# Attention of two sequences' same heads issued as couples: five full score groups instead of six, and a new order of the steps around them

## The chip, the cores and the metric

The kernel runs on one core of a Trainium2 chip. The metric is the device time of one execution in microseconds (us): 2496.99 us is the median of three runs, from 2496.44 to 2498.13. PE is the matrix engine (PEld its weight loads), DVE the vector engine, ACT the scalar engine, POOL the GpSimd engine, SP the engine whose queue issues all the transfers here.

## What is computed

The input is x of shape 8 x 512 x 1024 (eight sequences of 512 tokens), all in float32.

```
x = x + layernorm(attention(layernorm(x)))
x = x + layernorm(x' @ weight.T + bias + lora(x')),   x' = layernorm(x)

attention: 16 heads of 64; q, k with rotary embedding; causal mask
logits = q k^T / sqrt(64); attn = softmax(logits); out = attn v; out @ Wo
```

The change concerns the softmax part only: scores, exponentials, normalisation, transposition of the probabilities, and their product with the values.

## The kernel before

All large products (q and k, v, Wo, the feed-forward weight) are done with a seven-product scheme for 2 x 2 blocks (`PRODUCTS`, `GROUPS`). The kernel has four stages: values for all sequences; the q and k projections with attention beside them; the output product; the feed-forward product. The middle stage is the one that the change touches.

**Ticks.** The middle stage has eight units (`u` = 0 to 7: a group of 8 heads times two sequences). A unit has 49 ticks (`N2`). In each tick PE does one product of the projection, four matmuls of 256 columns (8 records in the trace, L636), and the accumulators are drained by DVE and ACT one tick later (`drain`, L116, L118, L125). Everything else is put on the ticks by `at(tick, fn, kind)`. `run` (L177) sets the order inside a tick: first all "pe" entries in the order in which they were registered, then the projection's product with its drain, then all other entries and the "post" entries, again as registered. Every engine's queue is in that written order. `plan_unit` registers ahead of the attention of the same unit.

**plan_unit** puts on DVE and POOL the sums that finish the projection (`add_cu`, L654) and the rotary embedding (`rotate`: L672 and L675 on DVE, L678 on POOL, then transfers to `qk`, L687). For units 1 to 6 the DVE sums stand on ticks 43 (A += D, first half), 44 (D += E first half, A += D second half), 45 (D += E second half), 50 and 51; the DVE steps of `rotate` on ticks 38 to 41, 46 to 49, 52 to 55 and 57 to 60, the POOL steps on 42, 50, 56 and 61.

**Pair** is the attention of two heads of one sequence. A unit has eight pairs; pair n is heads couple i = n // 2 of sequence s = n % 2. Its steps, for the query blocks qb = 0 to 3 of 128 rows (row block qb sees qb + 1 key blocks):

- `load`: a transfer of v into one of three buffers.
- `scores` (L747): matmuls of 64 rows into one PSUM tile of 2 heads x 512 columns. There is one such tile, so the next group has to wait until DVE has read the last one.
- `exps`: for each block and head DVE subtracts the maximum and copies to SBUF (L768), ACT takes the exponential and its sum (L778).
- `scale`: DVE takes reciprocals (L786), ACT multiplies (L792).
- `transpose` (L806) into one PSUM bank per head (two banks), and `keep` (L817, L818, L821): copies to `pT`, one head's on ACT, the other's on DVE.
- `values` (L827) on PE, then `store` (L842) on DVE.

The blocks go in three groups: (0, 1) with 128 + 256 = 384 columns, (2) with 384, (3) with 512. `Pair.plan` puts them relative to the pair's base tick: scores and exps at 0, 2, 4; scale at 4, 6, 8; transpose and keep at 6, 8, 10; values and store at 12; the load at -4. The eight pairs of a unit start six or seven ticks apart, from tick 10 of the next unit (12 in unit 1), so pair n's transposes share ticks with pair n + 1's scores. In unit 7 the pairs stand closer, and the last unit's attention runs after the projections (`alone`); these use the same `Pair.plan` before and after.

Beside it the SP queue loads the two operands of each product eight ticks ahead (`load_slot`, a ring of nine), and POOL prepares the later weights (`plan_part`, L562).

Of the kernel before, what the change touches and what calls it, by code (L numbers as in the profile page):

```python
# [10 lines left out]
F32 = mybir.dt.float32  # L11
I32 = mybir.dt.int32
AF = mybir.ActivationFunctionType
ALU = mybir.AluOpType
# [3 lines left out]
P = 128  # L18
B, S, E = 8, 512, 1024
HEADS, HD = 16, 64  # L20
NT = S // P
NK = E // P
NH = NK // 2
# [109 lines left out]
def sandwich_kernel(  # L133
# [15 lines left out]
    nc = tc.nc  # L149
# [44 lines left out]
    def at(tick, fn, kind=None):  # L194
        events[tick].append((kind, fn) if kind else fn)
# [525 lines left out]

    ops = {}

    class Pair:


        def __init__(self, u, n):
            self.u = u
            self.i, self.s = divmod(n, 2)
            self.g, bp = divmod(u, B // 2)  # L730
            self.b = 2 * bp + self.s
            self.name = f"{u}_{n}"
            self.pr, self.sm, self.ps = {}, {}, {}

        def load(self):
            self.v = work2["v"].tile([P, NT, P], F32, tag="v", name=f"v_{self.name}")
            nc.sync.dma_start(out=self.v, in_=vd[self.b][:, :, ts(NH * self.g + self.i, P)])

        def scores(self, qbs):
            qT, kT = (qk[self.u, self.i][:, :, self.s, w] for w in range(2))  # L740
            ps = ps_s.tile([P, 2, S], F32, tag="s", name=f"s_{self.name}_{qbs[0]}")
            at = 0
            for qb in qbs:
                L = (qb + 1) * P
                for j in range(2):
                    r = slice(j * HD, (j + 1) * HD)
                    nc.tensor.matmul(  # L747
                        ps[:, j, at : at + L],
                        lhsT=qT[r, qb],
                        rhs=kT[r, : qb + 1],  # L750
                        start=True,
                        stop=True,
                    )
                self.ps[qb] = ps[:, :, at : at + L]
                at += L

        def exps(self, qbs):
            pr = work2["work"].tile([P, 2, S], F32, tag="pr", bufs=4, name=f"pr_{self.name}_{qbs[0]}")
            at = 0
            for qb in qbs:  # L760
                L = (qb + 1) * P
                v = self.pr[qb] = pr[:, :, at : at + L]
                at += L
                nm = work2["small"].tile([P, 2], F32, tag="nm", name=f"nm_{self.name}_{qb}")
                sm = self.sm[qb] = work2["small"].tile([P, 2], F32, tag="sm", name=f"sm_{self.name}_{qb}")
                for j in range(2):

                    nc.vector.tensor_tensor_reduce(  # L768
                        out=v[:, j, :],
                        in0=self.ps[qb][:, j, :],  # L770
                        in1=work2["mask"][:, S - L :],
                        scale=-1.0 / HD**0.5,
                        scalar=3.0e38,
                        op0=ALU.add,
                        op1=ALU.min,
                        accum_out=nm[:, j : j + 1],
                    )
                    nc.scalar.activation(  # L778
                        v[:, j, :], v[:, j, :], AF.Exp,
                        bias=nm[:, j : j + 1], scale=-1.0, accum_out=sm[:, j : j + 1],  # L780
                    )

        def scale(self, qbs):
            for qb in qbs:
# [7 lines left out]
                        nc.scalar.mul(v, v, rs[:, j : j + 1])  # L792

        def transpose(self, qbs):
            if qbs[0] == 0:
                self.pT = [
                    work2["work"].tile([P, NT, S], F32, tag="pT", name=f"pT_{self.name}_{j}")
                    for j in range(2)
                ]
            self.pt = []  # L800
            for j in range(2):
                pt = ps_t.tile([P, NT, P], F32, tag="tp", name=f"ptp_{self.name}_{qbs[0]}_{j}")
                n = 0
                for qb in qbs:
                    for kb in range(qb + 1):
                        nc.tensor.transpose(pt[:, n, :], self.pr[qb][:, j, ts(kb, P)], ident)  # L806
                        n += 1
                self.pt.append(pt)

        def keep(self, qbs):  # L810
            for j in range(2):

                n = self.u * PAIRS + 2 * self.i + self.s - (UQ - 1) * PAIRS
                act = -2 <= n < 1 or j == 0 and (n < 0 or qbs[0] != 2)
                copy = nc.scalar.copy if act else nc.vector.tensor_copy
                if qbs[0] == 0:
                    copy(self.pT[j][:, 0, 0 : 2 * P], self.pt[j][:, 0:2, :])  # L817
                    copy(self.pT[j][:, 1, P : 2 * P], self.pt[j][:, 2, :])  # L818
                else:
                    (qb,) = qbs  # L820
                    copy(self.pT[j][:, : qb + 1, ts(qb, P)], self.pt[j][:, : qb + 1, :])  # L821

        def values(self):
            self.po = po = ps_v.tile([P, S], F32, tag="v", name=f"po_{self.name}")
# [35 lines left out]
        def plan(self, base, last=12, alone=False):  # L860
# [16 lines left out]
            if self.i == NH - 1:  # L877
                for m, k in enumerate((0, 0, 0, 0, 1) if alone else (1, 2, 3, 4, 6)):
                    at(base + last + k, lambda m=m: self.sum(m))

    products(-B, B, lambda q: ORDER)
    psum.close()
    operands.close()
# [14 lines left out]

    def start_attention():
        stay.close()  # L900
        for name, bufs in (("small", 4), ("ops", 2), ("v", 3), ("work", 2), ("ac", 1), ("qk", 5), ("ch", 1)):
            to = {"ac": rows_qk, "qk": rows_qk, "ch": chunks}.get(name, phase_a)
            work2[name] = right(to, name, bufs)
        ac = work2["ac"]
        mask = work2["mask"] = ac.tile([P, S], F32, name="mask")
        nc.sync.dma_start(out=cos, in_=rope[0])
        nc.sync.dma_start(out=sin, in_=rope[1])
        nc.gpsimd.memset(mask, 0.0)
        nc.gpsimd.affine_select(
            out=mask[:, S - P :], in_=mask[:, S - P :], compare_op=ALU.is_ge, fill=MASK_VAL,  # L910
            base=0, pattern=[[-1, P]], channel_multiplier=1,
        )
        select_adapters(ac)
# [81 lines left out]
    for u in range(UQ + 1):  # L995
        base = u * N2
        if u < UQ:
            plan_unit(u, base)
        if 0 < u < UQ - 1:
            for n in range(PAIRS):  # L1000
                first = 10 if u > 1 else 12
                Pair(u - 1, n).plan(base + first + (n * (N2 + 10 - first) + PAIRS // 2) // PAIRS)
        elif u == UQ - 1:
            for n in range(PAIRS):
                Pair(u - 1, n).plan(base + 9 + 5 * n, last=11)
            for n in range(PAIRS):
                Pair(u, n).plan(base + 51 + 6 * n, alone=True)
        if u < UQ:
            for n in range(base, base + N2):
                run(n, lambda n=n: unit_product(n))  # L1010
        else:
            run(base, lambda: cur.drain(NP))
            for k in range(base + 1, base + 10):
                run(k, None)
            streams.close()
            chunks.close()

            wop, gp, cl = (tc.alloc_tile_pool(name=name, bufs=1) for name in ("w2", "g2", "cl"))
            env["cl"] = cl
            tl = tc.alloc_tile_pool(name="tl", bufs=1)  # L1020
            for k, n in (
                (10, "R11"), (10, "L11"), (15, "R12"), (17, "R22"), (21, "L12"), (24, "R21"), (31, "L22"), (42, "S1"),
            ):
                if n in ("R11", "R12", "R21", "R22"):
                    at(base + k, lambda n=n: load_right(gp, 0, n))
                else:
                    at(base + k, lambda n=n: load_sums(wop, "wo", n, n))
            for k, n in ((21, "T1"), (26, "T2"), (32, "T4"), (44, "T3")):
                for m in range(3):
                    at(base + k + m, lambda n=n, m=m: sum_right(gp, 0, n, nc.gpsimd, slice(m, m + 1)))  # L1030
            at(base + 57, next_roles)
            for n in ("R12", "R11", "R21"):
                at(base + 57, lambda n=n: load_right(gp, 1, n))
            at(base + 52, lambda: combine(0, "c11", "c11", "A", nc.vector))
            cur, ticks = None, [*range(20, 44, 3), *range(44, 57)]
            for k in range(10, 57):
                if k in (51, 56):
                    n = {51: "S2", 56: "S4"}[k]
                    load_sums(wop2, "wo", n, n)
                if k == 49:  # L1040
                    rows_qk.close()
                    wop2 = tc.alloc_tile_pool(name="w2b", bufs=1)
                    load_sums(wop2, "wo", "S3", "S3")
                if k in ticks:
                    run(base + k, lambda n=ticks.index(k): first_product(n))
                else:
                    run(base + k, None)
            cur.drain(NP)
            run_rest()
# [311 lines left out]
```

## Time and profile before

| | |
|---|---|
| median of three runs | 2496.99 us |
| span of the profiled execution | 2491.9 us |
| between that span and the median | 5.1 us (the profile gives no other time of its execution) |
| PE busy | 2394.2 us, 96% |
| DVE, POOL, ACT busy | 1744.9 (70%), 1490.5 (60%), 1094.4 us (44%) |
| transfers | 606 MB, 73.9% of the 16 engines' span |
| score matmuls L747 | 1024 records, 193.8 us |
| transposes L806 | 1280 records, 178.7 us |
| value matmuls L827 | 1024 records, 157.4 us |
| projection matmuls L636 | 3136 records, 760.0 us |
| granted PE clock, mean | 0.988 |

A row of the timeline gives start, length (both us), engine, line, operation, output and inputs, shape and how many records are merged; in brackets the idle time ahead of it and what ended that. PE matmuls overlap, so the distance between two starts is what a run of matmuls costs. A row of the windows gives the busy time of each engine in a stretch, with the granted PE clock as a share of full speed, the transfers' share of their engines and GB/s.

### The profile page before, as it was taken

How to read it: one execution, taken by the hardware profiler on the slowest of the kernel's cores; microseconds unless marked ns; L12 is line 12 of the kernel's file. 1: busy time of each engine (PE TensorE's matmuls, PEld its weight loads, DVE VectorE, ACT ScalarE, POOL GpSimd, SP SyncE). 2: the span in 40 equal slices, each digit the busy share in tenths (PEclk: the TensorE clock that was granted, in tenths of full speed). 3: DMA queues.
4: the chain of work that ended last, by engine and by line, in shares of the span. 5: the costliest groups of instructions: out<-in, count | busy, mean ns of one | idle time of the engine just before them, and what ended most of it. 6: DMA issues, size and time to landing. Idle time of an engine off the chain costs nothing. (4 is left out here: it accounts for less than half of the span.)

```text
span 2491.9 us, 37087 instructions
## 1 busy us (share of the span) xinstructions
PE 2394.2 (96%) x12192; PEld 1880.4 (75%) x12192; DVE 1744.9 (70%) x3849; ACT 1094.4 (44%) x2749; POOL 1490.5 (60%) x1119
## 2 busy tenths in 40 slices
PE   6999999999999999999999999899999999999997
PEld 4787887877677777777777776458888878888886
DVE  8777767475857759486775957766777777766676
ACT  3323331026555556555555565763444544222222
POOL 3878875215263454637465363426777687888885
PEclk8999999999999999999999999899999999999999
DMA  7697787999899898988989895657566676434334
GB/s 261 198 299 251 241 272 235 344 307 285 238 302 285 258 328 255 328 267 297 326 264 346 250 327 174 219 182 266 178 202 212 217 278 240 137 126 153 132 106 140
DMA packets 415665, 606.00 MB, mean 243 GB/s; under 512 B 127889, under 2 KB 243601, under 8 KB 410866
## 3 DMA queue, kind: packets, MB, share of 16 engines
q1 hardware_dynamic: 415474, 603.64, 73.9%
q8 instruction: 98, 1.61, 0.3%
q14 instruction: 93, 0.76, 0.1%
HBM read 368.65 MB, written 201.33 MB: 229 GB/s over the span
## 5 line engine op out<-in xcount | busy, mean ns | idle before, releaser
L778 ACT ACTIVATE pr<-pr,nm 128x128 f32<-128x128 f32 (+3 forms) x512 | 280.9, 550 | 169.7 <-DVE nm L768 169.6
L792 ACT ACTIVATE pr<-pr,rs 128x128 f32<-128x128 f32 (+2 forms) x500 | 245.2, 549 | 119.9 <-DVE rs L786 119.8
L768 DVE CUSTOM_DVE_ANT_0 pr<-s,mask 128x128 f32<-128x128 f32 (+3 forms) x512 | 224.1, 484 | 41.8 <-PE s L747 39.7
L636 PE MATMUL acca_q_P<-xs,ls 128*128 128x256 f32 x896 | 217.3, 385 | 0.8 <-issue 0.8
L636 PE MATMUL accc_q_P<-xs,ls 128*128 128x256 f32 x896 | 217.7, 386 | 0.0
L636 PE MATMUL accb_q_P<-xs,ls 128*128 128x256 f32 x896 | 216.3, 384 | 0.8 <-DVE u_q_P L116 0.8
L1107 POOL TENSOR_TENSOR c<-c,row 128x512 f32<-128x512 f32 x120 | 160.7, 1360 | 87.4 <-ACT c L415 80.3
L636 PEld LDWEIGHTS acca_q_P<-xs,ls 128*128 128x128 f32 x896 | 165.3, 190 | 49.9 <-issue 19.1
L636 PEld LDWEIGHTS accc_q_P<-xs,ls 128*128 128x128 f32 x896 | 165.8, 190 | 48.4 <-issue 23.2
L636 PEld LDWEIGHTS accb_q_P<-xs,ls 128*128 128x128 f32 x896 | 165.4, 190 | 44.9 <-issue 6.2
L275 POOL TENSOR_TENSOR T<-R,T 128x512 f32<-128x512 f32 (+1 forms) x96 | 174.1, 1840 | 41.4 <-DVE u_P L337 21.0
L747 PE MATMUL s<-qk 64*128 64x128 f32 (+3 forms) x1024 | 193.8, 474 | 5.1 <-DVE nm L768 4.7
L806 PE MATMUL ptp<-ident,pr 128*128 128x128 f32 x1280 | 178.7, 278 | 11.0 <-DVE nm L768 4.8
L806 PEld LDWEIGHTS ptp<-ident,pr 128*128 128x128 f32 x1280 | 147.7, 142 | 43.1 <-ACT pr L792 15.8
L827 PE MATMUL po<-pT,v 128*64 128x512 f32 (+3 forms) x1024 | 157.4, 446 | 9.7 <-ACT pT L821 9.7
L562 POOL TENSOR_TENSOR wc_g<-wc_g 128x256 f32<-128x256 f32 (+1 forms) x120 | 124.1, 1053 | 65.5 <-DMA wc_g<-in_wqk_dram 43.5
L678 POOL TENSOR_TENSOR B_q<-B_q,m 128x1024 f32<-128x1024 f32 x14 | 35.0, 2497 | 199.0 <-DVE B_q L675 199.0
L827 PEld LDWEIGHTS po<-pT,v 128*64 128x64 f32 x1024 | 72.4, 139 | 102.0 <-issue 66.5
L337 DVE TENSOR_TENSOR p_P<-accb_P,p_P 128x256 f32<-128x256 f32 x109 | 45.0, 413 | 102.4 <-PE accb_P L315 53.5
L636 PE MATMUL accd_q_P<-xs,ls 128*128 128x256 f32 x448 | 108.7, 385 | 0.0
L337 DVE TENSOR_TENSOR u_P<-accb_P,p_P 128x256 f32<-128x256 f32 x109 | 46.1, 423 | 89.1 <-ACT p_P L342 89.0
L747 PEld LDWEIGHTS s<-qk 64*128 64x128 f32 x1024 | 73.1, 187 | 46.2 <-issue 27.9
(1108 smaller groups left out, 5809.7 us busy)
## 6 DMA issues: line engine op xcount, KB each, us to landing
ls<-wqk SPq DMA_DIRECT2D x392, 256.0 KB, 4.9
xs<-xop SPq DMA_DIRECT2D x392, 256.0 KB, 5.2
R<-attn SPq DMA_DIRECT2D x32, 896.0 KB, 5.5
wqk<-wc_g SPq DMA_DIRECT2D x16, 1568.0 KB, 9.3
x<-in_x_dram SPq DMA_DIRECT2D x32, 512.0 KB, 9.5
v<-vd SPq DMA_DIRECT2D x64, 256.0 KB, 5.0
attn<-ops SPq DMA_DIRECT2D x16, 1024.0 KB, 7.8
row<-in_x_dram SPq DMA_DIRECT2D x32, 512.0 KB, 5.9
```

The lines of the kernel that those rows point to most:

```text
L275: eng.tensor_tensor(RX[q, n][:, c], RX[q, x][:, c], RX[q, y][:, c], op=ALU.subtract)
L337: add = lambda out, x, a: nc.vector.tensor_tensor(out, acc[a], x, op=ALU.add)
L562: eng.tensor_tensor(out, x, y, op=op)
L636: nc.tensor.matmul(acc[:, :, w, :], lhsT=ls[:, k, w, :], rhs=xs_[:, :, k, :], start=(first and w == 0 and k == 0), stop=True, skip_group_c ...
L678: eng.tensor_tensor(v, v, m[step - 4, q], op=ALU.add)
L747: nc.tensor.matmul(ps[:, j, at : at + L], lhsT=qT[r, qb], rhs=kT[r, : qb + 1], start=True, stop=True,)
L768: nc.vector.tensor_tensor_reduce(out=v[:, j, :], in0=self.ps[qb][:, j, :], in1=work2["mask"][:, S - L :], scale=-1.0 / HD**0.5, scalar=3.0e38,
L778: nc.scalar.activation(v[:, j, :], v[:, j, :], AF.Exp, bias=nm[:, j : j + 1], scale=-1.0, accum_out=sm[:, j : j + 1],)
L792: nc.scalar.mul(v, v, rs[:, j : j + 1])
L806: nc.tensor.transpose(pt[:, n, :], self.pr[qb][:, j, ts(kb, P)], ident)
L827: nc.tensor.matmul(po[j * HD : (j + 1) * HD, kb * P :], lhsT=self.v[:, kb, ts(j, HD)], rhs=self.pT[j][:, kb, kb * P :], start=(kb == 0), s ...
L1107: nc.gpsimd.tensor_tensor(c, c, row[q, t][:, ts(h, HALF)], op=ALU.add)
```

## The change

`scores` and `exps` become functions over a list of (pair, block). The new `plan_couple` plans both sequences' pairs of the same heads, a and b, together, with five score groups of 512 columns each: blocks 1 of both; blocks 0 and 2 of a; block 3 of a; blocks 0 and 2 of b; block 3 of b. Transposes of a pair go in the groups (1), (0, 2), (3). A couple lasts 12 or 13 ticks; `values` of the last couple is registered ahead of the next one's scores, so it comes first in the tick that they share. The probabilities of both blocks 1 get a buffer pool of their own (`pr1`, two buffers of 4 KB a partition). `pT` is now taken in `keep`. It holds for the attention of units 0 to 5 (24 couples); the pairs of units 6 and 7 keep `Pair.plan`.

```diff
+    def scores(parts):
+        p, qb = parts[0]
+        ps = ps_s.tile([P, 2, S], F32, tag="s", name=f"s_{p.name}_{qb}")
+        at = 0
+        for p, qb in parts:
...
+                nc.tensor.matmul(
+                    ps[:, j, at : at + L], lhsT=qT[r, qb], rhs=kT[r, : qb + 1], start=True, stop=True
+                )
...
+    def exps(parts):
+        p, qb = parts[0]
+        pool, bufs = (work2["work"], 4) if qb != 1 else (work2["pr1"], 2)
+        pr = pool.tile([P, 2, S], F32, tag="pr", bufs=bufs, name=f"pr_{p.name}_{qb}")
...
         def keep(self, qbs):
+            if not self.pT:
+                self.pT = [
...
-                act = -2 <= n < 1 or j == 0 and (n < 0 or qbs[0] != 2)
+                act = -2 <= n < 1 or j == 0 and (n < 0 or qbs[0] not in (1, 2))
...
-                    (qb,) = qbs
-                    copy(self.pT[j][:, : qb + 1, ts(qb, P)], self.pt[j][:, : qb + 1, :])
+                    n = 0
+                    for qb in qbs:
+                        copy(self.pT[j][:, : qb + 1, ts(qb, P)], self.pt[j][:, n : n + qb + 1, :])
+                        n += qb + 1
...
+    def plan_couple(u, i, base, after):
+        a, b = (Pair(u, 2 * i + s) for s in range(2))
+        for p in (a, b):
+            at(base - 4 + 5 * p.s, p.load)
+        for p, k in ((a, after), (b, after + 5)):
+            at(k, p.values, "pe")
+            at(k, lambda _, p=p: p.store(), "post")
+            if i == NH - 1:
+                for m, n in enumerate((1, 2, 3, 4, 6)):
+                    at(k + n, lambda p=p, m=m: p.sum(m))
+        for k, m, p, qbs in (
+            (6, 4, a, (1,)), (8, 6, a, (0, 2)), (10, 9, a, (3,)),
+            (13, 11, b, (1,)), (14, 12, b, (0, 2)), (15, 13, b, (3,)),
+        ):
+            at(base + m, lambda p=p, qbs=qbs: p.scale(qbs))
+            at(base + k, lambda p=p, qbs=qbs: p.transpose(qbs), "pe")
+            at(base + k, lambda _, p=p, qbs=qbs: p.keep(qbs), "post")
+        for k, parts in (
+            (0, [(a, 1), (b, 1)]), (2, [(a, 0), (a, 2)]), (5, [(a, 3)]), (7, [(b, 0), (b, 2)]), (10, [(b, 3)]),
+        ):
+            at(base + k, lambda parts=parts: scores(parts), "pe")
+            at(base + k, lambda _, parts=parts: exps(parts), "post")
...
         if 0 < u < UQ - 1:
-            for n in range(PAIRS):
-                first = 10 if u > 1 else 12
-                Pair(u - 1, n).plan(base + first + (n * (N2 + 10 - first) + PAIRS // 2) // PAIRS)
+            first = 10 if u > 1 else 12
+            starts_ = [base + first + (n * (N2 + 10 - first) + 2) // 4 for n in range(5)]
+            for n in range(NH):
+                plan_couple(u - 1, n, starts_[n], starts_[n + 1])
```

So the four couples of a unit start on its ticks 10, 22, 35 and 47 (12, 24, 36 and 47 in unit 1), and the next unit's first on 59, which is its own tick 10.

More of the change, by code (lines that the diff above doesn't have):

```diff
@@ L722, in sandwich_kernel @@
     ops = {}
+    def scores(parts):
[3 more added lines that the diff above has]
+        for p, qb in parts:
+            qT, kT = (qk[p.u, p.i][:, :, p.s, w] for w in range(2))
+            L = (qb + 1) * P
+            for j in range(2):
+                r = slice(j * HD, (j + 1) * HD)
+                nc.tensor.matmul(
+                    ps[:, j, at : at + L], lhsT=qT[r, qb], rhs=kT[r, : qb + 1], start=True, stop=True
+                )
+            p.ps[qb] = ps[:, :, at : at + L]
+            at += L
+    def exps(parts):
+        p, qb = parts[0]
+        pool, bufs = (work2["work"], 4) if qb != 1 else (work2["pr1"], 2)
+        pr = pool.tile([P, 2, S], F32, tag="pr", bufs=bufs, name=f"pr_{p.name}_{qb}")
+        at = 0
+        for p, qb in parts:
+            L = (qb + 1) * P
+            v = p.pr[qb] = pr[:, :, at : at + L]
+            at += L
+            nm = work2["small"].tile([P, 2], F32, tag="nm", name=f"nm_{p.name}_{qb}")
+            sm = p.sm[qb] = work2["small"].tile([P, 2], F32, tag="sm", name=f"sm_{p.name}_{qb}")
+            for j in range(2):
+                nc.vector.tensor_tensor_reduce(
+                    out=v[:, j, :],
+                    in0=p.ps[qb][:, j, :],
+                    in1=work2["mask"][:, S - L :],
+                    scale=-1.0 / HD**0.5,
+                    scalar=3.0e38,
+                    op0=ALU.add,
+                    op1=ALU.min,
+                    accum_out=nm[:, j : j + 1],
+                )
+                nc.scalar.activation(
+                    v[:, j, :], v[:, j, :], AF.Exp,
+                    bias=nm[:, j : j + 1], scale=-1.0, accum_out=sm[:, j : j + 1],
+                )
     class Pair:
@@ L732, in __init__ @@
             self.name = f"{u}_{n}"
-            self.pr, self.sm, self.ps = {}, {}, {}
+            self.pr, self.sm, self.ps, self.pT = {}, {}, {}, None
         def load(self):
@@ L739, in scores @@
         def scores(self, qbs):
[L740 to L755, printed above, removed]
-        def exps(self, qbs):
[L758 to L781, printed above, removed]
+            scores([(self, qb) for qb in qbs])
+        def exps(self, qbs):
+            exps([(self, qb) for qb in qbs])
         def scale(self, qbs):
@@ L794, in transpose @@
         def transpose(self, qbs):
[L795 to L799, printed above, removed]
             self.pt = []
@@ L810, in keep @@
         def keep(self, qbs):
+            if not self.pT:
+                self.pT = [
+                    work2["work"].tile([P, NT, S], F32, tag="pT", name=f"pT_{self.name}_{j}")
+                    for j in range(2)
+                ]
             for j in range(2):
                 n = self.u * PAIRS + 2 * self.i + self.s - (UQ - 1) * PAIRS
-                act = -2 <= n < 1 or j == 0 and (n < 0 or qbs[0] != 2)
+                act = -2 <= n < 1 or j == 0 and (n < 0 or qbs[0] not in (1, 2))
                 copy = nc.scalar.copy if act else nc.vector.tensor_copy
-                if qbs[0] == 0:
+                if qbs == (0, 1):
                     copy(self.pT[j][:, 0, 0 : 2 * P], self.pt[j][:, 0:2, :])
@@ L900, in start_attention @@
         stay.close()
-        for name, bufs in (("small", 4), ("ops", 2), ("v", 3), ("work", 2), ("ac", 1), ("qk", 5), ("ch", 1)):
-            to = {"ac": rows_qk, "qk": rows_qk, "ch": chunks}.get(name, phase_a)
+        for name, bufs in (("small", 4), ("ops", 2), ("v", 3), ("work", 2), ("ac", 1), ("qk", 5), ("ch", 1), ("pr1", 2)):
+            to = {"ac": rows_qk, "qk": rows_qk, "ch": chunks, "pr1": chunks}.get(name, phase_a)
             work2[name] = right(to, name, bufs)
```

## Prediction

> **What bounds the kernel now.** I read the page first, then the windows by unit, then PE's timeline through the units that the change covers, then DVE's and POOL's timeline where DVE is fullest, and last PE's waits in the whole trace.
>
> ```profile
> span 2491.9 us, 37087 instructions
> PE 2394.2 (96%) x12192; PEld 1880.4 (75%) x12192; DVE 1744.9 (70%) x3849; ACT 1094.4 (44%) x2749; POOL 1490.5 (60%) x1119
> ```
>
> ```profile
> 963.00:1112.00 149.00, 148.91 (x810) 107.96 (x809) 106.13 (x258) 85.69 (x238) 81.97 (x56) 1.00 0.90 298
> 1008.00:1023.00 15.00, 15.00 (x81) 10.70 (x81) 6.51 (x18) 8.20 (x22) 4.39 (x5) 1.00 0.93 314
> 1083.00:1098.00 15.00, 15.00 (x79) 10.83 (x79) 14.43 (x25) 9.58 (x27) 3.37 (x2) 1.00 0.89 268
> ```
>
> Columns: length, busy time of PE, PEld, DVE, ACT and POOL, then clock, transfer share and GB/s. In a unit of 149 us PE never stops and the clock is full: the bound is PE's own stream, and only fewer or cheaper PE runs can shorten it. DVE is 71% busy over the unit, but unevenly: 6.5 of 15 us in one stretch, 14.4 of 15 in another. That second stretch is where the sums and the rotation stand (ticks 38 to 60), and PE passes it now without a gap.
>
> ```profile
> 1081.57 1.99 PE L636 MATMUL accc_q_P<-xs,ls 128*128 128x256 f32 x8
> 1083.40 1.89 PE L636 MATMUL acca_q_P<-xs,ls 128*128 128x256 f32 x8
> 1085.13 0.82 PE L806 MATMUL ptp<-ident,pr 128*128 128x128 f32 x6
> 1085.88 0.92 PE L747 MATMUL s<-qk 64*128 64x384 f32 x4
> 1086.72 1.99 PE L636 MATMUL accb_q_P<-xs,ls 128*128 128x256 f32 x8
> 1088.55 1.89 PE L636 MATMUL accc_q_P<-xs,ls 128*128 128x256 f32 x8
> 1090.28 1.04 PE L806 MATMUL ptp<-ident,pr 128*128 128x128 f32 x8
> 1091.25 1.13 PE L747 MATMUL s<-qk 64*128 64x512 f32 x4
> ```
>
> The starts give prices: a projection tick 1.73; 1.83 straight after scores; transposes 0.1075 each, plus 0.10 ahead of scores (0.75 for six, 0.97 for eight); a score group 0.84 to 0.86 for 384 columns and 1.06 for 512. The row at 1083.40 is tick 42, 1090.28 is in tick 45. Elsewhere in the same view a value block costs 2.30, a tick ahead of scores or values 0.09 more, and a transpose between two projection ticks nothing beyond its 0.1075 each.
>
> **What PE saves.** Matmuls, transposes and copies are as many as before, with the same shapes. Per unit, 24 score groups of together 8 x (0.855 + 0.845 + 1.06) = 22.1 us become 20 x 1.06 = 21.2: -0.9. Switches: before, a pair has one tick with values, transposes and scores (0.09 + 0.05 + 0.10 + 0.10 = 0.35) and two with transposes and scores (0.20 each), 8 x 0.75 = 6.0. After, scores or values stand in 20 ticks of a unit, 19 at 0.20 and one at 0.35, 4.1; the transposes that now stand alone cost no switch: -1.9. As a test, the same prices give before 49 x 1.727 + 160 x 0.1075 + 22.1 + 8 x 2.305 + 6.0 = 148.3, and units 4 and 5 lie 148.7 apart in the trace. So -2.8 us per unit, six units (1 to 6): **-16.7 us**, if nothing makes PE wait.
>
> **What PE waits for anew.** Before, each scale stands two ticks ahead of its transposes. Now it is two ticks in five of the six groups, and one tick for block 3 of a: scale at 9, transpose at 10. In the third couple (base 35) that is scale on tick 44, transposes first on PE on tick 45. Tick 44's entries of plan_unit come first: two sums on DVE ahead of the reciprocal. The trace of before has just these instructions:
>
> ```profile
> 1081.69 2.36 POOL L678 TENSOR_TENSOR B_q<-B_q,m 128x1024 f32<-128x1024 f32 x1 [6.08 <-DVE B_q L675]
> 1084.01 2.36 POOL L678 TENSOR_TENSOR F_q<-F_q,m 128x1024 f32<-128x1024 f32 x1
> 1084.40 3.06 DVE L654 TENSOR_TENSOR A_q<-A_q,D_q 128x1024 f32<-128x1024 f32 x1
> 1089.46 1.21 DVE L654 TENSOR_TENSOR D_q<-D_q,E_q 128x1024 f32<-128x1024 f32 x1
> 1090.60 1.21 DVE L654 TENSOR_TENSOR A_q<-A_q,D_q 128x1024 f32<-128x1024 f32 x1
> ```
>
> Tick 44's sums end at 1091.8, while tick 45's transposes start at 1090.28: a reciprocal behind them is late already by this row. The walk for after, from the start of tick 42's projection product. PE: 1.83 + transposes 0.86 + 1.73 + 1.73 = 6.15. DVE: exps of blocks 0 and 2 from 0.15, 2 x 0.21 + 2 x 0.475, to 1.54 (the rotation's last step ended 2.9 earlier, as now, so POOL's two additions still run); A += D beside POOL 3.06, to 4.6; the copies of tick 43, 0.66; the drain, 0.6; two sums, 2.4; reciprocal 0.15: 8.35. ACT's scaling of 512 columns 0.72 with hand-overs: 9.15. Wait 3.0 us. The same A += D took 3.43, 3.44, 3.06, 3.33 and 3.25 in units 2 to 6, so on the mean 3.2. In unit 1 (base 36: scale 45, transpose 46) the sums of 44 have a tick more, and the sum was 1.2: about 1.6. Together 5 x 3.2 + 1.6 = **+17.6 us**. Bounds: the add could meet an idle POOL (1.2 instead of 3.06), then 1.1 each and 7 in all; or another queue entry is late, 4 each and 22.
>
> **What such waits do to the clock.**
>
> ```profile
> 1546.62 0.93 PE L747 MATMUL s<-qk 64*128 64x128 f32 x8 [1.88 <-DVE nm L768]
> 1547.00:1550.00 3.00, 3.00 (x16) 1.77 (x14) 3.00 (x4) 2.35 (x7) 0.00 (x0) 1.00 0.86 197
> ...
> 1566.90 4.22 PE L827 MATMUL po<-pT,v 128*64 128x512 f32 x16 [2.61 <-ACT pT L821]
> 1567.00:1570.00 3.00, 3.00 (x9) 1.77 (x11) 2.93 (x3) 0.33 (x1) 0.00 (x0) 0.50 0.88 198
> ```
>
> Here a timeline row of PE and a window of the time just after it stand together. After the wait of 2.61 us (as after 2.57, 2.68, 2.96 and 4.79 elsewhere) PE's clock, the third number from the end, is 0.50 or on its way there, for some 3.4 us or twice that; after 1.88 it is 1.00. PE at half speed for 3.4 us loses 1.7; the value block at 1566.90 took 1.84 more than its 2.30. For five waits of 3.2: **+8.5 us**, with bounds of 0 (none trips) and 17 (6.8 us each).
>
> [...]
>
> **Transposes in consecutive ticks.** The three groups of b stand at 13, 14, 15, so the second needs DVE's copy of the first a tick earlier, where before it had two. In the fourth couple (base 47) these are ticks 60 to 62. From the end of tick 59's product DVE has two drains (0.2 to 1.5), a rotation step (1.14, or 2.06 beside POOL, as at 1139.99) and the copy 0.34: 3.0 or 4.0. PE wants the bank after 0.43 + 1.73 + 0.43 = 2.6. So 0.45 in three units and 1.4 in the three whose POOL works on weights then: **+5.5 us** (0 to 8). In the third couple the walk gives the bank free at the moment it is wanted, in the others DVE has no rotation there.
>
> **Edits with no cost.** The block-3 scale of the first couple (tick 19) has an ACT drain ahead of it: it is done 0.3 us before PE wants it, in the second couple a whole tick before, in the fourth 0.1 late; if a transfer of D to qk holds the drain, as it did for 0.8 us at tick 18, up to 1 us per unit goes on top. One scores tile: groups are two or three ticks apart, DVE reads one in 1.4 us, so no wait. v loads on SP: one at -4, one at +1; the reused buffer is read one tick before, and the ring of operands stands eight ticks (some 24 us) ahead with 5 us to landing, so SP's order costs nothing. Transfers are at 0.90; a unit 2.8 us shorter would need 0.92. The wait of 4.79 us at 562 comes from a transfer to qk and stays.
>
> **Sum.** -16.7 + 17.6 + 8.5 + 5.5 = +14.9. The profiled execution's span of 2491.9 goes to 2506.8; 5.1 lie around it to the median of the runs, so 2511.9. I take 2511.
>
> **Rivals.**
> 1. *The block-3 wait is not there*: DVE or ACT is far enough ahead of PE that only small waits remain. Below 1 us per unit there is no clock loss, and the time is -16.7 + 6 + 3: about 2489; wholly hidden, 2480. It decides at a wait of about 2 us per unit: 6 x 2 + 5 = 17. For it: PE passes ticks 38 to 60 today without a gap. Against: 1091.8 is after 1090.28.
> 2. *The waits are there but the clock stays up*: -16.7 + 17.6 + 5.5, 2503. For it: 1.88 kept the clock. Against: all five waits above 2.5 lost it.
> 3. *DVE becomes the bound of the stretch*: its rows of ticks 38 to 60 add up to some 71 us, against 69.8 us of PE now (23 ticks of 148.7 / 49) and some 67 after, so lateness passes from couple to couple, and the first couple's block 3 is late too: 1 to 2 us per unit more, and halvings of 6.8 us: 2525. Against: a PE wait lets DVE catch up.
>
> **How the numbers follow.** Forecast (2505 to 2519) 0.42, rival 1 0.26, rival 2 (2497 to 2505) 0.18, rival 3 0.14. 2511 is the forecast's time. 2484 to 2526 leaves out the ends of rivals 1 and 3. A measurement of this kernel tells 0.2%, 5 us, from no change. Rival 1 with its wait just under the deciding point (0.02) and half of rival 2 fall within it: faster 0.25, same 0.11, slower 0.64.
>
> **What would show it.** Right: PE idle ahead of transposes, released by ACT's scaling (L792), of some 3 us in units 2 to 6 at tick 45, and windows of clock 0.50 after them; distances between units near 151 instead of 148.7; between the waits, score rows of 512 columns only and projection runs unbroken by switches. Wrong: units of 146 us with clock 1.00 (rival 1), or waits on DVE spread over the whole stretch (rival 3). What would make it wrong above all is DVE's order in ticks 43 to 45 differing from the walk.

## The result and the profile after

The changed kernel takes 2512.37 us (median of four runs, 2506.43 to 2514.51), the kernel before in the same comparison 2497.56 (2496.44 to 2503.07). The ratio on record is 1.0048, with a 95% interval of 1.0031 to 1.0065 (the two medians give 1.0059, inside it): slower by half a per cent, and 1.4 us from the forecast of 2511.

The page of the changed kernel, first the span, then the busy times:

```profile
span 2508.7 us, 36924 instructions
PE 2386.2 (95%) x12192; PEld 1878.4 (75%) x12192; DVE 1732.7 (69%) x3849; ACT 1093.5 (44%) x2749; POOL 1496.3 (60%) x1119
```

PE is busy 8.0 us less than before, in a span that is 16.8 longer. So PE does have less to do, and what was won, and more, went into standing still. Up to the first rows of the output product the new trace is 14.75 us behind (1694.93 against 1680.18); the forecast's sum spoke of that stretch and said 14.9. The stage itself lost more: its first product starts at 429.79 us, against 431.75 before, so from there to the output product it takes 1265.14 us instead of 1248.43, 16.7 more. The 1.96 us ahead of it belong to code that is the same in both kernels.

The waits view of PE between 672 and 1440 us (five of the six units that have couples) names the places. Columns: who waited for whom, us in total, times, the longest.

```profile
PE ptp L808 <- ACT pr L799: 14.0, 6, 2.7
PE ptp L808 <- DVE pT L829: 3.8, 5, 1.3
```

Before, PE idled 0.09 us in the 738 us from 672 to 1410. Now it waits eleven times: five times for the scaling of the third couple's block 3 of a (tick 45), once for a scaling on tick 41, five times for DVE's copies on tick 61.

The windows of the changed kernel, with the same columns as in the prediction and, in the first two rows, the same stretches:

```profile
963.00:1112.00 149.00, 145.61 (x804) 106.47 (x803) 101.64 (x256) 84.50 (x236) 82.04 (x57) 1.00 0.89 296
1083.00:1098.00 15.00, 12.71 (x67) 9.41 (x66) 12.06 (x27) 8.63 (x25) 5.71 (x2) 1.00 1.02 311
```

In the second stretch PE has lost 2.29 us and DVE is busy for 12.06 of 15 us instead of 14.43: DVE is not full there, so what PE waits for is the order of DVE's queue. PE's timeline shows the place in unit 4:

```profile
1087.06 1.04 PE L808 MATMUL ptp<-ident,pr 128*128 128x128 f32 x8
1087.94 1.89 PE L636 MATMUL accb_q_P<-xs,ls 128*128 128x256 f32 x8
1089.67 1.89 PE L636 MATMUL accc_q_P<-xs,ls 128*128 128x256 f32 x8
1093.84 1.27 PE L808 MATMUL ptp<-ident,pr 128*128 128x128 f32 x8 [2.29 <-ACT pr L799]
1095.04 1.13 PE L734 MATMUL s<-qk 64*128 64x512 f32 x4
```

The first four rows are the transposes and product of tick 43, the product of tick 44, and tick 45's transposes. PE idles 2.29 us and is released by ACT's scaling. DVE and ACT in the same time:

```profile
1086.88 1.21 DVE L654 TENSOR_TENSOR A_q<-A_q,D_q 128x1024 f32<-128x1024 f32 x1
1088.14 0.76 DVE L829 COPY pT<-ptp 128x128 f32<-128x128 f32 x2
1089.94 0.69 DVE L116 TENSOR_TENSOR u_q_P<-accb_q_P,p_q_P 128x512 f32<-128x512 f32 x1 [1.04 <-PE accb_q_P L636]
1090.54 1.22 DVE L654 TENSOR_TENSOR D_q<-D_q,E_q 128x1024 f32<-128x1024 f32 x1
1091.68 1.22 DVE L654 TENSOR_TENSOR A_q<-A_q,D_q 128x1024 f32<-128x1024 f32 x1
1092.81 0.16 DVE L793 RECIPROCAL rs<-sm 128x2 f32<-128x2 f32 x1
1093.07 1.33 ACT L799 ACTIVATE pr<-pr,rs 128x512 f32<-128x512 f32 x2 [3.43 <-DVE rs L793]
```

The chain is the one of the prediction: drain, two sums, reciprocal, scaling, transposes. One thing in it is not: in this unit DVE was not behind. It stood idle for 1.04 us ahead of the drain, because the drain reads tick 43's product, and PE had not finished it (unit 6 is the same; in units 2 and 3 DVE goes into the drain without a gap). From there on everything is in a row, 3.9 us from the drain's start to the transposes, against one projection tick of 1.73 that PE has to do meanwhile.

Two such waits with what followed, PE's timeline in unit 2 and unit 3:

```profile
792.18 1.73 PE L808 MATMUL ptp<-ident,pr 128*128 128x128 f32 x8 [2.70 <-ACT pr L799]
943.56 1.27 PE L808 MATMUL ptp<-ident,pr 128*128 128x128 f32 x8 [2.69 <-ACT pr L799]
```

and the windows after these two, and after the waits of 2.74 and 2.28 in units 5 and 6 (the clock is the third number from the end):

```profile
792.30:795.70 3.40, 3.40 (x12) 1.58 (x12) 0.89 (x2) 1.03 (x2) 0.00 (x0) 0.53 0.96 238
944.00:947.00 3.00, 3.00 (x16) 1.78 (x14) 1.76 (x4) 1.04 (x3) 0.00 (x0) 1.00 0.93 215
...
1247.00:1250.00 3.00, 3.00 (x12) 2.04 (x12) 0.98 (x2) 1.12 (x2) 0.00 (x0) 0.50 1.01 204
1400.00:1403.00 3.00, 3.00 (x12) 1.94 (x12) 0.94 (x2) 1.08 (x2) 0.00 (x0) 0.51 1.03 187
```

The clock halves after three of the five waits: for 3.4 us in unit 2, 6.8 in unit 5 and 3.4 in unit 6. A wait of 2.70 brings it down and one of 2.69 does not; one of 2.28 (unit 6) brings it down and one of 2.29 (unit 4, the stretch shown above with 1.00) does not.

What differs is where a wait lies. By the trace's record of the granted clock it falls at 792.48, 1246.46 and 1400.06 us and stays at half speed for 3.413, 6.827 and 3.413 us. The falls are 133.0 and 45.0 times 3.413 us apart, and the nine other falls in this trace lie on the same grid (the one at 560.38 us is 68.0 cells ahead of the first). The waits of 2.70 and 2.28 us lie inside one cell of the grid, and 2.23 us of the one of 2.74 do. A line of the grid cuts the one of 2.69 at 942.67 into 1.80 and 0.89 us, and the one of 2.29 at 1092.85 into 1.30 and 0.99.

### The profile page after: what moved, and what is told of

It reads as the page before. It is cut to its first block, busy times and chain, and to the rows that moved or that the text cites. A ratio compares the mean times of both kernels' runs of the same rounds, so it can differ in the third digit from the quotient of the medians.

```text
span 2508.7 us, 36924 instructions
## 1 busy us (share of the span) xinstructions
PE 2386.2 (95%) x12192; PEld 1878.4 (75%) x12192; DVE 1732.7 (69%) x3849; ACT 1093.5 (44%) x2749; POOL 1496.3 (60%) x1119
## 5 line engine op out<-in xcount | busy, mean ns | idle before, releaser
L764 ACT ACTIVATE pr<-pr,nm 128x512 f32<-128x512 f32 (+3 forms) x512 | 281.7, 553 | 174.5 <-DVE nm L754 169.8
L799 ACT ACTIVATE pr<-pr,rs 128x256 f32<-128x256 f32 (+2 forms) x500 | 246.0, 551 | 231.5 <-DVE rs L793 231.3
L754 DVE CUSTOM_DVE_ANT_0 pr<-s,mask 128x512 f32<-128x512 f32 (+3 forms) x512 | 223.5, 486 | 73.4 <-PE s L734 71.4
L734 PE MATMUL s<-qk 64*128 64x256 f32 (+3 forms) x1024 | 188.5, 472 | 6.3 <-DVE nm L754 5.1
L829 DVE COPY pT<-ptp 128x256 f32<-128x256 f32 (+2 forms) x225 | 108.3, 502 | 47.5 <-PE ptp L808 46.2
```

The costliest lines, as they stand in the source:

```text
L734: nc.tensor.matmul(ps[:, j, at : at + L], lhsT=qT[r, qb], rhs=kT[r, : qb + 1], start=True, stop=True)
L754: nc.vector.tensor_tensor_reduce(out=v[:, j, :], in0=p.ps[qb][:, j, :], in1=work2["mask"][:, S - L :], scale=-1.0 / HD**0.5, scalar=3.0e38 ...
L764: nc.scalar.activation(v[:, j, :], v[:, j, :], AF.Exp, bias=nm[:, j : j + 1], scale=-1.0, accum_out=sm[:, j : j + 1],)
L829: copy(self.pT[j][:, : qb + 1, ts(qb, P)], self.pt[j][:, n : n + qb + 1, :])
```

## The experiments

My theory: PE's saving is real, and the scaling of block 3 that stands one tick ahead of its transposes, behind two DVE sums, eats it, through the wait and the clock. The rivals: DVE has too much to do in the stretch, so that the wait only moves; or the couples' order on PE costs time by itself. All ratios are against the kernel before in the same comparison.

**The scaling one tick earlier (on tick 43 of the third couple).**

```diff
-            (6, 4, a, (1,)), (8, 6, a, (0, 2)), (10, 9, a, (3,)),
+            (6, 4, a, (1,)), (8, 6, a, (0, 2)), (10, 8, a, (3,)),
```

> The changed kernel with one number altered: the scaling of block 3 of a stands at tick 8 of the couple instead of 9, so two ticks ahead of its transposes like all others. Theory (the late reciprocal on tick 44 is the main loss): the six waits ahead of the third couple's transposes, together 14.2 us in the profile of the change, fall below 2 us together, and with them most of the halved clock (6.8 us lost) goes: about 20 us less than the changed kernel, 2490 to 2494, which is below the time before (2497). Rival (DVE is full over ticks 38 to 60, the wait only moves): other waits on DVE or ACT of 1 to 2 us per unit come up in the same stretch, less than 10 us gained, 2503 or more. Rival (PE saves next to nothing by the new order): the waits go, but the time does not fall below 2497.

Measured: 2491.3 us, against 2495.88 for the kernel before; ratio 0.9976 (0.9964 to 0.9988). One number in the code turns the slower kernel into one that is faster than before. PE's timeline at the same place:

```profile
1085.82 1.89 PE L636 MATMUL accc_q_P<-xs,ls 128*128 128x256 f32 x8
1087.54 1.04 PE L808 MATMUL ptp<-ident,pr 128*128 128x128 f32 x8
1088.51 1.13 PE L734 MATMUL s<-qk 64*128 64x512 f32 x4
```

Transposes start 1.72 us after the product and take 0.97, with no wait; none of the units 2 to 6 has one here (unit 1 has one of 0.34), and the clock does not halve (the score groups behind run 1.13 us, as above). The waits that are left, in the same stretch as above:

```profile
PE ptp L808 <- ACT pr L799: 3.1, 3, 1.3
PE ptp L808 <- ACT pT L829: 2.5, 7, 0.7
PE ptp L808 <- DVE pT L829: 1.6, 5, 0.6
PE accd_q_P L636 <- DVE p_q_P L116: 0.9, 1, 0.9
```

They are 8.1 us in sixteen small pieces. The profiled execution took 2495.37 us, 4 more than the median of the ten, and in it the stage takes 1248.49 us, as long as before (1248.43). So this trace shows that the loss is gone; the gain over before stands on the medians and the interval.

**The same scaling on its old tick, but ahead of the two sums.** Here nothing moves to another tick: the two sums of tick 44 are registered behind the couples' entries, so the reciprocal comes first in DVE's queue.

```diff
-            at(base + k, lambda out=out, x=x, i=i: add_cu(u, out, x, i, dve))
+            put = late_.append if k == 44 else lambda e: at(*e)
+            put((base + k, lambda out=out, x=x, i=i: add_cu(u, out, x, i, dve)))
...
+            while late_:
+                at(*late_.pop(0))
```

> The changed kernel with the scaling left on tick 9, but the two DVE sums of tick 44 are registered behind the couples' entries of that tick, so that the reciprocal stands ahead of them in DVE's queue; nothing else moves. Theory: the wait at tick 45 loses the two sums, 2.3 us, in units 2 to 6 (0.5 us or less is left) and the clock stays up there; unit 1, where the scaling is on tick 45, keeps its 1.5: some 16 to 18 us less than the changed kernel, 2494 to 2497. If the one tick of distance by itself, and not the sums, is what hurts, the waits shrink by less than half and the time stays above 2503.

Measured: 2493.74 us; ratio 0.9996 (0.998 to 1.0011). DVE's timeline in unit 4:

```profile
1087.67 0.69 DVE L116 TENSOR_TENSOR u_q_P<-accb_q_P,p_q_P 128x512 f32<-128x512 f32 x1 [0.67 <-PE accb_q_P L636]
1088.28 0.15 DVE L794 RECIPROCAL rs<-sm 128x2 f32<-128x2 f32 x1
1088.35 1.29 DVE L654 TENSOR_TENSOR D_q<-D_q,E_q 128x1024 f32<-128x1024 f32 x1
1089.57 1.21 DVE L654 TENSOR_TENSOR A_q<-A_q,D_q 128x1024 f32<-128x1024 f32 x1
```

and PE's:

```profile
1087.40 1.89 PE L636 MATMUL accc_q_P<-xs,ls 128*128 128x256 f32 x8
1089.31 1.27 PE L809 MATMUL ptp<-ident,pr 128*128 128x128 f32 x8
```

The waits at tick 45 are 0.49, 0.43, 0, 0, 0 us in units 2 to 6, none with a halved clock (behind the first two the score groups run 1.13 us): the same tick is nearly enough if the two sums are not ahead. The loss against before is gone. A gain over before is not shown: the copies' waits are longer than in the first experiment (4.4 us against 1.6), and unit 1 keeps a wait of 1.81.

**The same distance in the kernel before.** The scaling of block 3 goes from two ticks to one ahead of its transposes, for all eight pairs of a unit.

```diff
-                at(base + k - (4 if alone else 2), lambda qbs=qbs: self.scale(qbs))
+                at(base + k - (4 if alone else 1 if qbs == C3 and 0 <= self.u < UQ - 2 else 2), lambda qbs=qbs: self.scale(qbs))
```

> The kernel before with one alteration: in units 0 to 5's attention the scaling of block 3 stands one tick ahead of its transposes instead of two. Everything else, the six score groups included, is as before. Theory: PE, which never waited in units 2 to 6, now waits for ACT's scaling at tick 45 (some 2.6 us: the sums of tick 44 end at 1091.8, the transposes start at 1090.3, plus the reciprocal and the scaling) and some 1.4 us at tick 51, behind the sum on tick 50; with the clock that follows 4 to 6 us per unit, 2515 to 2535. If the waits of the change come from the couples' order as a whole and not from the distance of that scaling, the time stays within 3 us of before.

Measured: 2540.59 us; ratio 1.018 (1.0161 to 1.0199), more than expected. DVE's timeline in unit 3, then PE's:

```profile
956.39 0.68 DVE L116 TENSOR_TENSOR u_q_P<-accb_q_P,p_q_P 128x512 f32<-128x512 f32 x1
956.99 1.21 DVE L654 TENSOR_TENSOR D_q<-D_q,E_q 128x1024 f32<-128x1024 f32 x1
958.12 1.21 DVE L654 TENSOR_TENSOR A_q<-A_q,D_q 128x1024 f32<-128x1024 f32 x1
959.26 0.15 DVE L786 RECIPROCAL rs<-sm 128x2 f32<-128x2 f32 x1
```

```profile
955.76 1.89 PE L636 MATMUL accc_q_P<-xs,ls 128*128 128x256 f32 x8
960.22 1.27 PE L806 MATMUL ptp<-ident,pr 128*128 128x128 f32 x8 [2.58 <-ACT pr L792]
961.42 2.08 PE L747 MATMUL s<-qk 64*128 64x512 f32 x4
```

The old kernel, given this distance, shows the same chain and 2.57 to 2.58 us of wait on the same tick, so the couples are not needed for the loss. Each unit has two more waits, 1.12 us at tick 51 (1.4 was expected) and 0.6 at another pair, which the expectation left out; unit 1 has two of 1.74 and 3.25. Behind the waits of 2.57 to 2.58 the clock is 0.57 and 0.53 in the windows from 961 to 964 and from 1119 to 1122 us (the scores at 961.42 run 2.08 us instead of 1.13), and 1.00 in the one from 1431 to 1434. The units lie 156.4 to 157.4 us apart at the same tick, some 8 more than before, where 4 to 6 were expected.

**DVE's copies on tick 61 given to ACT.** In the changed kernel, for block 1 of b.

```diff
-                act = -2 <= n < 1 or j == 0 and (n < 0 or qbs[0] not in (1, 2))
+                act = -2 <= n < 1 or j == 0 and (n < 0 or qbs[0] not in (1, 2)) or qbs == (1,) and self.s == 1
```

> The changed kernel, but both heads' copies of b's block 1 go to ACT, so that the second of the three transposes in consecutive ticks no longer waits for DVE's copy behind its drains and rotation. Theory: the waits of 0.4 to 1.3 us released by DVE's copies at tick 61 (3.8 us together in units 2 to 7) go, ACT has the room (0.27 us more each time): 3 to 5 us less than the changed kernel, 2507 to 2510. If ACT is then late with these copies, the same waits appear with ACT as releaser and nothing is gained.

Measured: 2510.74 us; ratio 1.0057 (1.004 to 1.0074). No gain can be told from the changed kernel's 1.0048. The waits, same stretch:

```profile
PE ptp L808 <- ACT pr L799: 14.9, 6, 2.7
PE s L734 <- DVE nm L754: 1.8, 2, 1.1
PE accd_q_P L636 <- DVE p_q_P L116: 1.1, 1, 1.1
PE ptp L808 <- ACT pT L829: 0.4, 1, 0.4
```

The 3.8 us of waits for DVE's copies are gone, and 3.3 us of other waits have come: scores that wait until DVE has read the last group's tile, and a drain. But they do not stand on tick 61. The scores are on tick 29 of units 5 and 6, the drain on tick 40 of unit 6. Ahead of the first and of the last of them DVE's timeline has these rows:

```profile
1193.98 0.69 DVE L851 COPY ops<-po 128x512 f32<-128x512 f32 x1 [5.82 <-DMA attn<-ops]
1378.40 3.36 DVE L672 TENSOR_TENSOR m<-F_q,sin 128x1024 f32<-128x1024 f32 x1 [4.32 <-POOL F_q L654]
```

DVE stood idle both times, for 5.82 us until a transfer out of `ops` had ended and for 4.32 us until POOL had finished its sum F. So these waits come from a transfer and from POOL, not from the copies: the drain on tick 40 waits 0.91 us in the first experiment too, where DVE still has the copies, behind 4.12 us of idle time for the same sum. That the load moved from one instruction of DVE to the next is not shown; that the edit alone brought a gain is not shown either.

**Both edits: the scaling earlier, the copies on ACT.**

> The scaling of block 3 of a at tick 8 and both copies of b's block 1 on ACT together. If the two terms are separate losses, their gains add: the DVE waits at tick 61 that are left in the first (0.2 to 0.6 us a unit) go as well, 1 to 3 us below the run with the scaling alone (2491.3), 2488 to 2490. If the load only passes from DVE to ACT, waits released by ACT's copies replace them and the time is the same or higher.

Measured: 2488.9 us (before: 2498.1); ratio 0.9963 (0.995 to 0.9977). Best so far by its median, but the intervals of this and of the earlier scaling alone overlap. ACT's copies are now waited for nine times, 3.4 us in all, where in the first experiment ACT's and DVE's together were waited for twelve times, 4.1 us.

**Six score groups instead of five.** The earlier scaling, and the first group (both blocks 1, 512 columns) split in two of 256 on two ticks.

```diff
-            (0, [(a, 1), (b, 1)]), (2, [(a, 0), (a, 2)]), (5, [(a, 3)]), (7, [(b, 0), (b, 2)]), (10, [(b, 3)]),
+            (0, [(a, 1)]), (1, [(b, 1)]), (2, [(a, 0), (a, 2)]), (5, [(a, 3)]), (7, [(b, 0), (b, 2)]), (10, [(b, 3)]),
```

> The scaling of block 3 of a at tick 8, and the first full score group of a couple (blocks 1 of both sequences, 512 columns) parted into two of 256 columns on ticks 0 and 1, so that a couple has six score groups as before the change; all else as in the run with the scaling alone (2491.3). Theory (PE's saving is the number of score groups and of switches around them): a group more costs 2 x 0.64 - 1.07 = 0.2 us by 0.205 us of fixed cost each, and the tick that now holds scores costs 0.2 in switches, 0.4 us x 24 couples = 10 us: 2499 to 2503. If full groups as such are worth nothing and the gain is all in where the transposes stand, 2490 to 2493.

Measured: 2493.77 us; ratio 0.9983 (0.9969 to 0.9996). A half costs PE 0.64 us, so two cost 0.21 more than the one of 1.07, and there is a switch more: PE's prices are as the prediction had them. The time rises less than expected, and a rise over the first experiment (0.9976) cannot be told from none. In the two profiled executions the waits fall at once, from 8.1 to 2.8 us in the same stretch (1.8 for scalings, 0.8 for a copy on ACT, 0.2 for a drain). By these two traces, waits for DVE and ACT take back a part of what five groups save on PE.

**The scaling of a's block 1 two ticks earlier**, on top of the first experiment, against the wait on tick 41.

```diff
-            (6, 4, a, (1,)), (8, 6, a, (0, 2)), (10, 9, a, (3,)),
+            (6, 2, a, (1,)), (8, 6, a, (0, 2)), (10, 8, a, (3,)),
```

> The scaling of block 3 of a at tick 8 and that of block 1 of a at tick 2 instead of 4, so that its reciprocal stands ahead of the first rotation step beside POOL (tick 38) in the third couple. Theory: the waits of 0.6 to 1.25 us at tick 41 in units 4 to 6 go, 1 to 3 us below the run with block 3 alone (2491.3): 2488 to 2490. If DVE's lateness in that stretch is what counts, the copies and sums behind it wait instead and nothing is gained.

Measured: 2491.45 us; ratio 0.9969 (0.9956 to 0.9982): no gain over the first experiment that could be measured. The scaling's waits fall from 3.1 to 0.9 us, and there are 1.1 us for scores and 4.8 instead of 4.1 for copies. The longest for scores, 0.91 us, is on tick 29 of unit 5, behind 5.67 us in which DVE stood idle for a transfer out of `ops`, so it did not come from the edit by way of DVE's load.

**Scores ahead of values** in the ticks that they share, on top of the first experiment: `values` is registered behind the couples' scores.

```diff
-        for p, k in ((a, after), (b, after + 5)):
-            at(k, p.values, "pe")
...
+        held.append((a, b, i, after))
...
+            plan_values()
```

> The scaling of block 3 of a at tick 8, and in the ticks where values of the last couple and scores of the next meet, scores first and values behind them (the order of the change undone). PE's work is the same, DVE gets two of the five score groups of a couple 2.3 us earlier, the copies of the values later. Theory (PE is the bound and the short waits left come from DVE's queue between drains and rotation): within 3 us of the run with block 3 alone, 2488 to 2494. If the order of values and scores carries part of the loss or gain, it moves by more.

Measured: 2490.16 us; ratio 0.9967 (0.9957 to 0.9976). Units 3 to 5 take 147.1 to 148.3 us from start to start, units 2 and 6 148.7 and 150.0. PE's cost does not change (1.06 us for a score group and 2.30 for a value block in either order), while the exponentials of those ticks can start earlier by a value block, 2.30 us. A gain over the first experiment alone is not shown.

**The last two together.**

> The change with block 3 of a scaled at tick 8, block 1 of a at tick 2, and scores ahead of values in shared ticks. If the last waits of units 2 to 6 (tick 41 behind the scaling of block 1, up to 1.25 us; tick 61 behind DVE's copy, 0.4 to 0.9) each come from their own cause, the first kind goes and the time is 1 to 2 us below that with scores first alone (2490.2), 2487 to 2490 and 8 to 10 us below before. If they hang together through DVE's load, it is the same as that run.

Measured: 2489.97 us (before: 2497.65); ratio 0.9961 (0.9947 to 0.9975). The same again, within the intervals.

**Scaling earlier, copies on ACT, scores first.**

> The change with block 3 of a scaled at tick 8, scores ahead of values in shared ticks, and both copies of b's block 1 on ACT. With scores first the exponentials of a couple's first group reach ACT 2.3 us earlier, so ACT has room for the second copy at tick 60: the waits at tick 61 (0.4 to 0.9 us a unit) go without ACT's own taking their place, 2486 to 2490, 8 to 11 us below before. If ACT is late instead, 2490 or more.

Measured: 2488.02 us (before: 2497.65); ratio 0.996 (0.9947 to 0.9972), the lowest median of all: 0.4% faster than the kernel before, and by the two ratios (0.996 / 1.0048) 0.9% faster than the changed one. Its waits in the same stretch:

```profile
PE ptp L808 <- ACT pr L799: 2.7, 4, 1.2
PE accd_q_P L636 <- DVE p_q_P L116: 1.0, 1, 1.0
PE ptp L808 <- ACT pT L829: 0.6, 2, 0.5
PE accb_q_P L636 <- DMA xs<-xop: 0.4, 1, 0.4
```

In this execution 4.7 us of waits are left, of the changed kernel's 17.8 and the first experiment's 8.1, and 0.6 of them are for copies on ACT. That the time is below the first experiment's is not shown: the intervals overlap.

## Why the prediction was right, and by how much its terms were off

The direction, the cause and the place were right. That the number came so close was in part luck. Within the stage 16.7 us were lost, not 14.9, and the 14.75 of the whole trace come about because the unchanged code ahead of it took 1.96 us less in this execution. And all four predicted terms turned out smaller than predicted, while some 6 us came that were not predicted. Term by term, for the stage up to the output product:

| term | predicted | measured | how measured |
|---|---|---|---|
| PE's saving | -16.7 | -15.7 | estimate from four units, rows matched: 594.85 to 607.88 us, of it 14.8 idle and 8.7 in rows that ran longer (half clock, or beside a wait), so -10.5, or -2.62 a unit; times 6 |
| waits at tick 45 | +17.6 | +14.2 | 1.48, 2.70, 2.69, 2.29, 2.74, 2.28 in units 1 to 6 |
| halved clock | +8.5 | +6.8 | 13.6 us at half speed |
| copies on tick 61 | +5.5 | +3.8 | 0.38, 0.37, 1.10, 1.29, 0.65 |
| not predicted: waits elsewhere | 0 | +2.0 | 1.25 on tick 41 of unit 5; 0.21 and 0.55 in unit 1; 0.81 in unit 7; 0.65 more at some 561 us; less 0.89, 0.20 and 0.36 that the kernel before had in unit 1 |
| not predicted: rows beside a wait run longer | 0 | +2.9 | estimate: some 0.24 each (behind the waits of units 3 and 4 the eight transposes took 1.20 from start to start, without a wait 0.97) for the twelve waits of units 1 to 6 in the rows above (6 at tick 45, 5 on tick 61, 1 on tick 41) |
| not predicted: transposes on tick 57 | 0 | +1.4 | 1.20 instead of 0.97 in each of six units, with no wait in the view (see the last part) |
| sum | +14.9 | +15.4 | the trace has 16.7; 1.3 stay unassigned |

*PE's saving.* Right in its prices: the scores' groups cost 1.06 to 1.07 each, switches and transposes what the rows of before said. Off by 0.16 a unit.

*Waits at tick 45.* The mis-sized term: 2.54 on the mean of units 2 to 6 instead of 3.2. The walk failed at "A += D beside POOL 3.06". In units 4, 5 and 6 that add ran in 1.21 to 1.22 us, and POOL's addition took the delay (unit 4):

```profile
1086.92 3.38 POOL L678 TENSOR_TENSOR F_q<-F_q,m 128x1024 f32<-128x1024 f32 x1
```

Before, POOL's row took 2.36 and DVE's 3.06. In these rows the one that began first was the short one: in units 4 to 6 DVE's add starts 0.04 to 0.06 us ahead of POOL's, which took 3.38 to 3.39. In units 2 and 3 POOL was 0.40 ahead and took 2.36 to 2.37, the add took 3.05 and 3.04, and the walk's 3.0 came out as 2.70 and 2.69.

The lower bound of this term ("the add could meet an idle POOL, then 1.1 each") failed for another reason. With the add at 1.21 the wait should have been 1.1 and was 2.29 in unit 4, since DVE cannot use the time it has won: the drain ahead of the two sums has to wait for tick 43's product. After that product 0.6 + 2.3 + 0.2 us of DVE and 0.7 of ACT with the hand-overs stand against PE's 1.73, whatever was before. (In unit 5 it was 2.74: the first of the two sums took 1.64 beside POOL's late addition.) The bound was a subtraction from the walk and forgot that the walk has a second input.

*The clock.* The term took all five waits; three halved the clock, 13.6 us at half speed. The rival that the clock stays up was right for two of them. Both went by the length of a wait; in these five the falls went with how the wait lay on the grid of 3.413 us (2.23 us or more of idle time in one cell, against 1.80 or less), so how many of them would count was chance.

*Copies on tick 61.* Right in kind and place, off in size: the walk's 0.45 and 1.4 were 0.37 to 0.38 in two units, 0.65 in one and 1.10 and 1.29 in two. That they were worth their length is not shown: with the copies on ACT they were gone, and no gain could be told.

*No-cost edits.* The scaling on tick 41 was not among the ones looked at: one wait of 1.25 us in unit 5, behind a rotation step that DVE could start only after 3.31 us of idle time, when POOL had finished its sum F, and that then took 3.36 us beside POOL. Of the list, the scaling of the fourth couple, "0.1 late", cost 0.23 us in each of six units. The other edits cost nothing that the trace shows, beyond 0.21 and 0.55 us in unit 1 and 0.81 in unit 7.

*The rivals.* The first, no wait at tick 45, gave 2489 (2480 if all of it were hidden). The first two experiments take the wait away: 2491.3 and 2493.74, 4.6 and 2.1 us below the kernel before in the same comparison, where the rival's sum said 8. So its sum was 3 to 6 us too good, and the distance of one tick behind two sums stands as the cause. The third, DVE as the bound, is refuted as the main thing: the same DVE work in another order brings waits of 0.49 us or less there. Nor do the new waits with the copies on ACT (1.06, 0.70 and 1.10 us) speak for it: ahead of each DVE had stood idle, for a transfer or for POOL's sum. The marks "near 151 us a unit" were 149.96, 150.28, 155.95 and 151.6 in units 3 to 6, and 153.82 in unit 2; the one of 155.95 has the 6.8 us at half speed.

## What to carry to other kernels

Where a step of a filled stream moves one tick closer to its consumer, walk what is registered ahead of it on the slower engine in that tick, from the last input that the stream itself delivers; this floor stays whatever else gets faster, and here waits of 2.54 us a unit, with what they did to the clock, ate a saving of 2.62 on PE. Of the further edits on top of the first experiment, none gave a gain over it that could be told (0.996 to 0.9983 against 0.9976, with intervals that overlap). Before a wait is put down to an engine that is nearly full, look at what that engine did just ahead of it: with the copies on ACT, DVE had stood idle for up to 5.82 us.

## What the runs showed of the hardware that was not expected

- Waits of PE of nearly one length did or did not halve its clock: three of five from 2.28 to 2.74 us in the changed kernel, for 3.4 or 6.8 us. In its trace, as in that of the kernel before, all falls lie on a grid of 3.413 us. By the most idle time that one cell of the grid got, these five waits part cleanly: 2.23, 2.28 and 2.70 us halved the clock, 1.30 and 1.80 did not. Elsewhere in the trace 1.70 in one cell did (the wait that ends at 1611.50 us), so the idle time is not all that counts.
- The length of a wait alone did not tell what it costs. The one of 1.88 us that the prediction read as harmless was cut by the grid of its trace into 1.54 and 0.34, and in the changed kernel, at 1559.48 us, into 1.00 and 0.88, with the clock at 1.00 after it both times. The one of 1.70 lay in one cell, and after it the clock was 0.50.
- Eight transposes that are released as soon as ACT has scaled the first of the two heads take 1.20 us from start to start of what follows, instead of 0.97, at full clock. PE's weight loads stop again until the second head is scaled, which the waits view of PE does not list; it happens after the waits at tick 45 and, with no wait in the view, on tick 57 of units 1 to 6. PEld in unit 4, behind the wait of 2.29:

```profile
1094.45 0.42 PEld L808 LDWEIGHTS ptp<-ident,pr 128*128 128x128 f32 x4 [0.20 <-ACT pr L799]
```

- Of two additions of 128x1024 on DVE and POOL at the same time, the one that started later was the longer: 1.21 us on DVE beside 3.38 on POOL with DVE first by 0.04 us (the changed kernel, unit 4), 3.06 on DVE beside 2.36 on POOL with POOL first by 0.39 (the kernel before, unit 4).
- Values ahead of scores or behind them: PE's cost of both is the same, 2.30 and 1.06 us; the difference is in when the exponentials can start.
